# Adding squared outputs to their running sums by an accumulating DMA from GpSimd, in place of GpSimd additions

## The chip, the cores and the metric

The kernel runs on one core of a Trainium2 chip. A core has five engines with queues of their own: TensorE (PE, with its weight loads shown apart as PEld), VectorE (DVE), ScalarE (ACT), GpSimd (POOL) and SyncE (SP, which here only issues DMAs). Sixteen DMA engines move data between the core's memory and HBM. The metric is device time in microseconds (us), the median over several executions. Everything is float32.

## The reference

The reference is one transformer layer on a batch of 2 sequences of 512 tokens with 512 features. A layernorm is followed by two branches that are added to the input: a linear attention with 32 heads of 128, and a base linear layer with a router over 8 low-rank experts. What matters here is the end of the attention branch:

```
attn = blocks of linear attention, heads side by side   # [2, 512, 32*128]
xf   = attn * rsqrt(mean(attn*attn, axis=-1) + EPS)     # mean over all 4096 features of a token
normed = norm_w * xf
gate = sigmoid(hidden @ gate_w.T)
return gate * normed @ out_w.T
```

The mean square of a token runs over all heads, so it is known only when the last head is done. The kernel therefore multiplies the un-normed outputs by `out_w`, sums the squares on the side, and scales the rows at the very end.

## The kernel before, in words

**Stages.** Up to some 45 us the layernorm, the router and the base layer run. After that come the projections as rounds of 7 by 7 smaller products (Strassen's scheme used twice): first the v and gate weights (to about 400 us), whose results go to HBM (`v_kept`, `gate_kept`), then the q and k weights. The attention of a (head, batch) pair starts when its q and k are complete and is woven between the rounds; the product with `out_w` begins within that stage and fills the rest, from about 939 us on.

**One attention item.** There are 64 items, one for each head and batch `b`. `attend` (L685 to L767) is a generator whose parts are run at fixed slots of the round loop (L894 to L960). Its steps are these. v is loaded (L691). The key tile is transposed in 32 by 32 squares by DVE (L697, L698), written to HBM (L702, `k_kept`) and read back as `kt` by four DMAs (L707): this completes the transposition. PE makes the scores (L715), DVE masks them (L720, L724), POOL makes `qd` (L727), and the gate is loaded (L731). ACT scales `kt` to `kd` (L736), PE multiplies `kd` and v (`ps_sc<-v,kd`, by the helper at L99), and DVE makes the states of the blocks (L744, L746). PE then makes the output `pa` in the one PSUM bank with the tag `at` (L749 to L754), and DVE multiplies it by the gate into `gT` (L756). ACT squares `pa` into `sq` (L763), and POOL adds `sq` to `ssq[b]` (L764). For the first item of each batch ACT writes the square into `ssq[b]` itself (L760), so the addition is done 62 times. Last, `gT` is written to HBM (L766, `g_kept`).

**Buffers.** `sq` has one buffer (`RING` at L83, "sq": (1, 1)) of 128 by 512 float32, 256 KB: the next Square may write only when the previous addition has read it. `ssq[0]` and `ssq[1]` are kept for the whole kernel. The items of a batch mostly come in pairs. The bank `at` is single too, so the next item's `pa` waits for this item's Square.

**What sets the order.** Between L372 and L1016 the order on PE, ACT, DVE, POOL and SP is the order in which the code is written; behind that the framework's planner orders the instructions itself. The framework sets the waits. An engine works its queue in order, so an instruction that waits holds up all that stands behind it. On POOL these are the operand sums of the rounds (`s` at L172 and L184, `e` at L191 to L197), `qd` and the sums of `out_w` (`wsum`, L834). All DMAs of this stage are issued by SP; POOL issues none.

**After the last item.** DVE transposes both `ssq` (L1035) and reduces them (L1036), SP sends the parts through HBM (L1038, L1040), and DVE and ACT make `rms`, which the `finish` steps use. DVE also makes the sums `gsum` (L833) that PE's last products read.

Of the kernel before, what the change touches and what calls it, by code (L numbers as in the profile page):

```python
# [37 lines left out]
ALU = mybir.AluOpType  # L38
# [23 lines left out]
def attn_moe_kernel(ctx: ExitStack, tc: tile.TileContext, x, qk_w, v_w, gate_w, out_w, norm_w,  # L62
                    decay, base_w, base_b, router_a_w, lora_b, out):
    nc = tc.nc
# [20 lines left out]
    def ring(tag, shape=None):  # L85
        n, bufs = RING[tag]
        return work.tile(shape or [P, n * 512], F32, tag=tag, name=tag, bufs=bufs)
# [14 lines left out]
    ssq = [keep.tile([P, S], F32, tag=f"ssq{b}", name=f"ssq{b}") for b in range(B)]  # L102
# [574 lines left out]
    def complete(item):  # L677

        items.append(item)
        g = running[len(items) - 1] = attend(*item)  # L680
        ready[len(items) - 1] = now[0] + 4
        for slots in (1, 2, 3, 6):
            later[now[0] + slots].append(g)

    def attend(head, b):  # L685
# [72 lines left out]
        if b not in seen:  # L758
            seen.add(b)
            nc.scalar.activation(ssq[b], pa, AF.Square)  # L760
        else:
            sq = ring("sq")
            nc.scalar.activation(sq, pa, AF.Square)  # L763
            nc.gpsimd.tensor_tensor(ssq[b], ssq[b], sq, ALU.add)  # L764
        yield
        nc.sync.dma_start(g_kept[head // 2][:, :, head % 2, b, :], gT.rearrange("p (f s) -> p f s", f=2))  # L766
        yield  # L767
# [399 lines left out]
```

## Time and profile before

| what | value |
|---|---|
| median of 3 runs | 1118.93 us (1117.61 to 1119.57) |
| the profiled execution | 1121.18 us, of it 1119.4 us span from first to last instruction |
| PE busy | 1106.9 us, 99% of the span |
| DVE, ACT, POOL busy | 773.3, 444.9, 765.7 us |
| the 62 additions on POOL (L764) | 79.2 us, 1277 ns each, the first at 441.5 us, the last at 939.4 us |
| the 62 Squares on ACT (L763) | 597 ns each |
| SP's queue of DMAs | 199.03 MB, 57.9% of 16 engines' span |
| DMA share from 441 to 939 us | 0.65 |

A group's row in the profile has the line, the engine, the operation, the tiles written and read, the shapes and the count; then busy time in us and the mean of one in ns; then the idle time of the engine just before these instructions, with what ended it. A row of the timeline has the start and the length in us, and in square brackets the idle time ahead of it and its releaser. SPq marks DMA issues of SP; their length is that of the issue, and the data land later.

### The profile page before, as it was taken

To read this page: it belongs to the slowest core of one execution; us is meant where nothing else is said; L and a number is where in the kernel's file an instruction comes from. 1 tells how busy PE (TensorE), PEld (TensorE's weight loads), DVE (VectorE), ACT (ScalarE), POOL (GpSimd) and SP (SyncE) were. 2 spreads that over 40 slices of the span, in tenths; PEclk is the share of its full clock that TensorE was granted. 3 is DMA by queue.
4 is the path that set the end of the run, shared out by engine and by line. 5 is a ranking of instruction groups with operands and counts; after the bars stand their busy time and mean duration, and the time that the engine had idled before them with its cause. 6 is when DMAs were issued, how large, how long until landed. Compare 5 with 4: busy or idle time off the path is not lost.

```text
span 1119.4 us, 30341 instructions
## 1 busy us (share of the span) xinstructions
PE 1106.9 (99%) x11984; PEld 849.9 (76%) x11984; DVE 773.3 (69%) x1535; ACT 444.9 (40%) x842; POOL 765.7 (68%) x825
## 2 busy tenths in 40 slices
PE   8999999999999999999999899999999999999998
PEld 7666777777777777777777678777777877777776
DVE  8777776676766668787877777778777786535424
ACT  4344444434444444444444443535444443410000
POOL 3568778779768776677687676777777667545542
PEclk9999999999999999999999999999999999999999
DMA  5534576776743546665665666657666677944221
GB/s 178 156 114 159 163 241 202 220 229 209 239 143 132 177 146 197 182 199 154 199 187 160 191 183 186 189 164 211 181 197 177 211 234 233 350 132 127 86 90 57
DMA packets 190925, 201.09 MB, mean 180 GB/s; under 512 B 53696, under 2 KB 163008, under 8 KB 190656
## 3 DMA queue, kind: packets, MB, share of 16 engines
q1 hardware_dynamic: 190640, 199.03, 57.9%
q8 instruction: 95, 1.56, 0.6%
q14 instruction: 46, 0.38, 0.1%
q10 hardware_dynamic: 144, 0.13, 0.0%
HBM read 128.79 MB, written 75.55 MB: 183 GB/s over the span
## 4 chain that ended last, share of the span: by engine, by line
PE 79%; DVE 10%; DMA 4%; issue 3%; ACT 3%; SPq 1%; POOL 1%; DVEq 0%; ACTq 0%; POOLq 0%
PE sd L99 28%; PE ps_fr L99 24%; PE ps_sc L99 17%; PE ps_at L99 8%; PE ps_sc L715 2%; DVE qk L537 2%; DVE sum L537 2%; DMA raw<-in_qk_w 1%; ACT sd L569 1%; ACT qk L514 1%; DVE w L552 1%; DMA k_kept<-squares 1%; DMA v<-v_kept 1%; DVE gT L756 1%; DVE y L552 0%
## 5 line engine op out<-in xcount | busy, mean ns | idle before, releaser
L99 PE MATMUL sd<-xt,e 128*64 128x256 f32 x1344 | 175.8, 379 | 0.0
L764 POOL TENSOR_TENSOR ssq<-ssq,sq 128x512 f32<-128x512 f32 x62 | 79.2, 1277 | 138.0 <-ACT sq L763 131.0
L514 ACT ACTIVATE qk<-qk 128x512 f32<-128x512 f32 x128 | 80.3, 630 | 203.5 <-DVE qk L537 203.5
L99 PEld LDWEIGHTS sd<-xt,e 128*64 128x64 f32 x1344 | 102.6, 137 | 35.3 <-issue 2.6
L552 DVE TENSOR_TENSOR w<-sd,sum 128x512 f32<-128x512 f32 x110 | 74.5, 690 | 61.0 <-ACT sd L569 60.9
L569 ACT COPY sd<-sd 128x512 f32<-128x512 f32 x112 | 64.2, 573 | 130.1 <-PE sd L99 106.5
L558 ACT COPY sd<-ps_fr 128x512 f32<-128x512 f32 x112 | 64.2, 573 | 72.3 <-PE ps_fr L99 71.2
L99 PE MATMUL ps_at<-scores,v 128*64 128x128 f32 x1024 | 89.6, 273 | 0.0
L834 POOL TENSOR_TENSOR wsum<-wo 128x256 f32<-128x256 f32 x48 | 38.5, 821 | 68.7 <-PE sd L99 28.6
L833 DVE TENSOR_TENSOR gsum<-gated 128x256 f32<-128x256 f32 x54 | 27.3, 546 | 80.9 <-PE ps_sc L99 57.4
L172 POOL TENSOR_TENSOR s<-raw 128x1024 f32<-128x1024 f32 x32 | 75.7, 2367 | 6.8 <-DMA raw<-in_v_w 3.3
L99 PE MATMUL ps_at<-qd,state 128*64 128x128 f32 x768 | 75.2, 273 | 0.0
L99 PE MATMUL ps_fr<-xsum,s 128*64 128x256 f32 x576 | 75.1, 379 | 0.0
L99 PEld LDWEIGHTS ps_at<-scores,v 128*64 128x64 f32 x1024 | 65.9, 138 | 9.1 <-issue 0.4
L756 DVE SCALAR_TENSOR_TENSOR gT<-gate,ps_at 128x512 f32<-128x512 f32 x64 | 43.7, 682 | 36.1 <-PE ps_at L99 34.4
L727 POOL TENSOR_TENSOR qd<-qk,mask 128x384 f32<-128x384 f32 x64 | 64.7, 1010 | 0.9 <-PE ps_at L99 0.9
L191 POOL TENSOR_TENSOR e<-s 128x256 f32<-128x256 f32 x64 | 46.7, 730 | 23.7 <-PE sd L99 21.4
L715 PEld LDWEIGHTS ps_sc<-qk 128*64 128x64 f32 x1024 | 53.6, 137 | 8.7
L763 ACT ACTIVATE sq<-ps_at 128x512 f32<-128x512 f32 x62 | 37.0, 597 | 55.5 <-DVE gT L756 55.5
L99 PE MATMUL sd<-e,xt 128*64 128x256 f32 x448 | 59.0, 379 | 0.0
L99 PE MATMUL ps_fr<-xt,e 128*64 128x256 f32 x440 | 57.7, 382 | 0.2 <-DVE qk L537 0.2
L191 POOL TENSOR_TENSOR e<-raw 128x256 f32<-128x256 f32 x48 | 36.1, 753 | 30.7 <-PE sd L99 30.7
(349 smaller groups left out, 2959.6 us busy)
## 6 DMA issues: line engine op xcount, KB each, us to landing
raw<-in_qk_w SPq DMA_DIRECT2D x64, 256.0 KB
v<-v_kept SPq DMA_DIRECT2D x64, 256.0 KB
gate<-gate_kept SPq DMA_DIRECT2D x64, 256.0 KB
g_kept<-gT SPq DMA_DIRECT2D x64, 256.0 KB
gated<-g_kept SPq DMA_DIRECT2D x27, 512.0 KB
k_kept<-squares SPq DMA_DIRECT2D x64, 192.0 KB
kt<-k_kept SPq DMA_DIRECT2D x256, 48.0 KB
gate_kept<-v SPq DMA_DIRECT2D x47, 256.0 KB
```

Source lines behind the costliest of these rows:

```text
L99: nc.tensor.matmul(o[h * HP : (h + 1) * HP], lhsT[:, of * HP : (of + 1) * HP], rhs, start=start, stop=stop, **more)
L172: nc.gpsimd.tensor_tensor(t, a, b, op)
L191: nc.gpsimd.tensor_tensor(e[:, 0], a21, a22, ALU.add)
L514: nc.scalar.activation(v, v, AF.Silu)
L537: engine.tensor_tensor(o, halves(v), halves(t), ALU.add)
L552: nc.vector.tensor_tensor(o, v, t, ALU.add)
L558: nc.scalar.copy(st["pb"], st["pa"])
L569: nc.scalar.copy(st["pd"], st["pb"])
L715: nc.tensor.matmul(pc[at * HP : (at + 1) * HP, asked], k[:, keys], q[:, asked], start=True, stop=True, skip_group_check=True)
L727: nc.gpsimd.tensor_tensor(qd, q[:, P:].rearrange("p (j n) -> p j n", j=TB - 1), mask[:, 3:5].rearrange("p h n -> p (h n)").unsqueeze(1).to ...
L756: nc.vector.scalar_tensor_tensor(gT, gate, 1.0, pa, ALU.add, ALU.mult)
L764: nc.gpsimd.tensor_tensor(ssq[b], ssq[b], sq, ALU.add)
```

## The change

For all items but the first of each batch, the POOL instruction that adds `sq` to `ssq[b]` is replaced by a DMA that POOL issues: the DMA engines read `sq`, read `ssq[b]`, and write the sum to `ssq[b]`. The Squares, the buffers and everything else stay as written.

```
         else:
             sq = ring("sq")
             nc.scalar.activation(sq, pa, AF.Square)
-            nc.gpsimd.tensor_tensor(ssq[b], ssq[b], sq, ALU.add)
+            nc.gpsimd.dma_start(ssq[b], sq, accum_op=ALU.add)
         yield
```

The DMA takes over the waits of the addition. It needs the Square that wrote `sq`, and the previous change of `ssq[b]`, which is now a DMA as well. What waited for the addition now waits for the landing of the DMA: the next Square (it reuses `sq`), and DVE's transposes of `ssq` after the last item.

More of the change, by code (lines that the diff above doesn't have):

```diff
@@ L763, in attend @@
             nc.scalar.activation(sq, pa, AF.Square)
-            nc.gpsimd.tensor_tensor(ssq[b], ssq[b], sq, ALU.add)
+            nc.gpsimd.dma_start(ssq[b], sq, accum_op=ALU.add)
         yield
```

## The prediction

> **What bounds the kernel now.** I read the page's busy times first, then the chain that ended last, then the waits of PE and of POOL, and last the timeline where PE does wait.
>
> ```profile
> PE 1106.9 (99%) x11984; PEld 849.9 (76%) x11984; DVE 773.3 (69%) x1535; ACT 444.9 (40%) x842; POOL 765.7 (68%) x825
> PE 79%; DVE 10%; DMA 4%; issue 3%; ACT 3%; SPq 1%; POOL 1%; DVEq 0%; ACTq 0%; POOLq 0%
> L764 POOL TENSOR_TENSOR ssq<-ssq,sq 128x512 f32<-128x512 f32 x62 | 79.2, 1277 | 138.0 <-ACT sq L763 131.0
> ```
>
> PE is the bound, and POOL is 1% of the chain. The third row is what goes: POOL spends 79.2 us on the additions and waits 138.0 us ahead of them for the Squares. POOL is early, so a faster POOL only waits longer. PE waits for POOL nowhere in the attention stage; the waits of PE from 441 to 939 us are these.
>
> ```profile
> PE ps_sc L99 <- ACT kd L736: 2.5, 1, 2.5
> PE ps_fr L99 <- ACT sd L558: 2.1, 7, 0.3
> ```
>
> The first is the only large one. It ends a chain of DMAs: `k_kept`, `kt`, then `kd` on ACT. The timeline shows it, SP first, then ACT, then PE.
>
> ```profile
> 624.47 0.55 SPq L702 DMA_DIRECT2D k_kept<-squares  x1
> ...
> 631.41 1.76 SPq L707 DMA_DIRECT2D kt<-k_kept  x4
> ```
> ```profile
> 635.12 0.80 ACT L736 ACTIVATE kd<-kt,mask 128x256 f32<-128x256 f32 x2 [3.63 <-DMA kt<-k_kept]
> ```
> ```profile
> 635.68 0.95 PE L99 MATMUL ps_sc<-v,kd 128*64 128x128 f32 x12 [2.51 <-ACT kd L736]
> ```
>
> `k_kept` took 6.9 us from issue to landing (SP sat until 631.41 for it), `kt` 3.6 more, and PE stood still. The chain repeats every 65.92 us (the double `qk` addition of DVE stands at 491.11, 557.03 and 622.95 us), but the next is at 693.35: this set took 70.40, a slip of 4.5 us for a gap of 2.5 to 3.0. The rest is the clock: from 636 to 640 us its granted share was 0.60.
>
> In other sets the same chain is just in time. By the recorded DMA semaphores `kt` lands at most 0.2 us ahead of its `kd` in 10 items, and the slack that is left to PE behind these is: 0.0 and 0.2 us (items near 566 and 574), 0.1 (622), none (635), 1.0 (643), 0.9 (709), 0.0 (768), 0.8 (841), 1.1 (907), 0.5 (930).
>
> **The change part by part.**
>
> *POOL.* Removed: 62 x 1.277 = 79.2 us. Added: 62 DMA issues, each of d us. No row shows a DMA issued by POOL. From below: SP's issue of `k_kept`, median 0.336 us. From above: the longest common POOL instruction, 128x1024 at 2.367 us. I take 1.0, an estimate between the two, nearer SP's as it is the same kind of work. Behind the issue on POOL stand `qd`, `e` and `wsum`. POOL idles 136.1/61 = 2.2 us ahead of each addition in this stage, which covers 2.367 - 1.277 = 1.1 more, so the cost is 0 at both ends. Were the cover gone, POOL (352.8 busy of 498 us, 77.9 of it these additions) would be full at 352.8 - 77.9 + 61d = 498, d = 3.7 us.
>
> *DMA traffic.* Added: 62 x 0.262 MB. SP's queue moved 199.03 MB in 57.9% of 16 engines' 1119.4 us, so 256 KB hold 16 engines for 0.85 us: the lower bound. The destination is read as well, so I double it for the upper, 1.7, and take 1.3. The stage's DMA share rises from 0.65 by 61 x 1.3/498 = 0.16 to 0.81. There is room on average; the price is paid where an accumulating DMA meets `k_kept` or `kt`. It does: the addition at 556.49 lies between the `k_kept` at 555.89 and its `kt` at 561.26, the one at 622.41 2.1 us ahead of the `k_kept` at 624.47, and those at 758.73 and 824.64 lie 0.6 and 1.3 us behind the `k_kept` at 758.09 and 823.33. SP's order doesn't protect the chain, since the new transfer comes from another queue.
>
> With a delay of 1.3 on each tight chain, less its slack, and counting a set once because a stall relieves what follows: 1.3 (566) + 1.3 (622, 635) + 0.4 (709) + 1.3 (768) + 0.5 (841) + 0.2 (907) + 0.8 (930) = 5.8 us. With 0.85: 0.85 x 3 + 0.35 = 2.9. With two meetings of 1.7, so 3.4: 3.4 + 3.4 + 2.5 + 3.4 + 2.6 + 2.3 + 2.9 = 20.5, and gaps of that length also cool the clock (1.5 to 2 us each as at 636), some 8 us more. Below: the timing of the one slip may also turn out well, minus 4.5.
>
> *The new waits.* The next Square waits until the DMA has landed, and the Squares are on ACT ahead of `kd`, `qk` and the scales. The latency L from issue to landing: from below the 16 KB of `part_kept`, issued at 944.22 and landed by 947.26, 3.0 us; from above `k_kept`'s 6.9. I take 4.5, which lies nearer the usual `k_kept` than its worst. In the steady stage Squares are 7.4 to 9.5 us apart, so the wait costs 0 up to L = 6.5 and under 0.4 beyond; PE's next use of the bank `at` is 3 us later (Square done at 556.42, next `pa` at 559.62). The wait of a DMA for the previous one on `ssq[b]` is covered by the same distance. At the end the items come closer:
>
> ```profile
> 931.58 0.60 ACT L763 ACTIVATE sq<-ps_at 128x512 f32<-128x512 f32 x1 [0.83 <-DVE gT L756]
> 935.50 0.60 ACT L763 ACTIVATE sq<-ps_at 128x512 f32<-128x512 f32 x1 [3.32 <-DVE gT L756]
> 938.75 0.60 ACT L763 ACTIVATE sq<-ps_at 128x512 f32<-128x512 f32 x1 [2.66 <-DVE gT L756]
> ```
> ```profile
> 936.14 0.44 PEld L99 LDWEIGHTS ps_at<-scores,v 128*64 128x64 f32 x8 [0.21 <-ACT sq L763]
> 941.32 1.30 DVE L1035 STREAM_TRANSPOSE turned<-ssq 128x512 f32<-128x512 f32 x2 [1.99 <-DMA g_kept<-gT]
> ```
>
> (the first fence is ACT, in the second PE's last item and DVE's transposes). The DMA of the item at 931.58 is issued at 932.26 and lands at 936.8, so the Square of 935.50 slips 1.3 us, and PE, which already waits for this Square without slack, slips the same 1.3. The last Square then waits for the next DMA, to 942.1, and its own DMA lands at 947.3. DVE's transposes stand at 947.3 in place of 941.3, 6.0 late, and with them the `gsum` queued behind. PE is itself 2.1 late by then (1.3, and 0.8 from the chain at 930), and the second of these `gsum`, ready at 944.6, was used at 947.03, so 2.5 us are covered: 6.0 - 2.1 - 2.5 = 1.4 us more stall. `wsum` behind POOL's last issue is late by about the same, beside it. Sum of the tail 1.3 + 1.4 = 2.7. With L = 3.0 it is 0. With L = 6.9 the Square slips 3.7, the transposes come at 954.3, and 13.0 - 3.7 - 2.5 = 6.8 follow: 10.5. The later way of the sums through HBM (`part_kept`, `rms`) isn't needed before the first `finish`, and costs 0; SP's `gated` and `wo` loads behind `part_kept` have some 5 us before their sums are used.
>
> *A rule against the row.* The row is `part_kept`, 3.0 us for 16 KB. The Trainium skill, DMA: Bandwidth & Descriptors, section Anatomy of one DMA, puts a DMA issued by GpSimd at about 2.0 us plus bytes over 436 GB/s, which would be 2.6 us here, an estimate; by it the tail is 0 and the sum 5.8. As the row for a sixteenth of the bytes is longer already, I keep the row. Speaking against the change, SBUF: State Buffer, section SBUF: two separate sides, says that DVE in its two-port modes keeps GpSimd from writing descriptors, 620 ns becoming some 3100 ns; no run here shows it, and 2.5 us more on L would make the tail nearly that of L = 6.9, for a sum of about 16.
>
> **Sum.** 0 + 5.8 + 2.7 = 8.5 us. The profiled execution took 1121.18 us, 2.25 above the median of the runs, so the sum is added to the median: 1118.93 + 8.5 = 1127.4 us, 0.8% slower.
>
> **The rivals.**
> 1. *The transfer is hidden.* DMA engines are 35% idle, and if the new packets fall between the others, the chains move by less than their slacks and L is near 3.0: within 2.2 us, 1119 us. Against it: three chains have no slack.
> 2. *Faster.* A shorter hold on POOL (0.34 for 1.28) ends `s` and `e` 0.9 us earlier, so raw weight buffers come free earlier, SP issues the loads at 622.50 and 623.84 earlier, and `k_kept` at 624.47 finds empty queues. From the point where `kt` lands 3.0 us earlier (632.0) the slip is gone: 1118.9 - 4.5 = 1114.4. Against it: the added bytes use the same engines, and 0.9 is not 3.0.
> 3. *POOL becomes the bound.* With d above 3.7; at d = 5, 61 x 1.3 = 79 us more, 1198. For it only that no row shows d.
> 4. *The queues back up.* Two meetings per chain, cold clock and L = 6.9: 20.5 + 8 + 10.5 = 39 us, 1158. For it: SP already waits 134.2 us for `k_kept`, so each delay holds back all its other loads.
>
> **How the numbers follow.** What can be told from no change is 0.2%, 2.2 us. Forecast (2 to 20 us slower) 0.60; rival 1 0.15; rival 2 0.08; rival 3 0.06; rival 4 0.11. Faster is rival 2, 0.08; same rival 1, 0.15; slower the rest, 0.77. The forecast's own range is 1121 to 1139. For 8 in 10 I leave out rival 3, rival 2 and the upper part of rival 4: 1117.5 to 1148.
>
> **What would show it.** POOL's idle ahead of what was L764, still some 2 us an item, and no PE wait on POOL. A new DMA queue with about 16 MB and a DMA share near 0.8 in the stage. More rows of `kd` waiting for `kt`, and of PE for `kd`, spaced 66 us, with the granted clock down behind them. Near 936 us a Square that waits for a DMA and PE for that Square, and `turned` waiting for the accumulation. It is wrong if PE waits for `qd` or `e` (d is large), if no new gap appears (the traffic is hidden), or if the gaps sit elsewhere.

## The result: 5.7% slower, and the profile after

The changed kernel takes 1182.58 us (median of 4 runs, 1181.06 to 1184.96) against 1118.37 us before (4 runs, 1117.61 to 1119.57): a ratio of 1.0574, 95% interval 1.0554 to 1.0594. The forecast was 1127.4 us and its range ended at 1148. The profiled execution took 1181.25 us with a span of 1179.4 us, 60.0 us more than the span before.

The page of the changed kernel: busy times, the queue of GpSimd's DMAs, the chain by engine, and the row of the issues (count | busy us, mean ns | idle before, releaser).

```profile
PE 1130.0 (96%) x11984; PEld 884.9 (75%) x11984; DVE 813.8 (69%) x1535; ACT 445.6 (38%) x842; POOL 741.2 (63%) x825
...
q0 software_dynamic: 8928, 16.26, 8.1%
...
PE 80%; DVE 10%; issue 3%; DMA 3%; ACT 2%; SPq 1%; POOL 1%; DVEq 0%; ACTq 0%; POOLq 0%
...
L764 POOL DMA_DIRECT2D ssq<-sq x62 | 54.5, 879 | 221.7 <-ACT sq L763 201.3
```

POOL has less to do and waits longer, as foreseen, and is still 1% of the chain. But DVE is 40.5 us busier, although the change touches no instruction of DVE's. The waits of PE (us in total, times, longest) say where that matters:

```profile
PE ps_fr L99 <- DVE qk L537: 35.6, 13, 4.5
PE ps_sc L99 <- ACT kd L736: 3.7, 2, 3.4
```

Before, the first of these was

```profile
PE ps_fr L99 <- DVE qk L537: 0.2, 1, 0.2
```

and the second, on which the forecast rested, has hardly moved (2.5 us in one wait). So the gaps are new ones, and they wait for `qk` of DVE. One form of `qk` accounts for it. These are the groups of DVE by form; first before, then after.

```profile
L537 DVE TENSOR_TENSOR qk<-w,sum 128x512 f32<-128x512 f32 x8 | 9.7, 1211 | 0.8
```
```profile
L537 DVE TENSOR_TENSOR qk<-w,sum 128x512 f32<-128x512 f32 x8 | 51.5, 6442 | 0.8
```

The same eight instructions take 41.8 us more, as much as all of DVE's extra time. They are the additions that `put` makes with `in_sbuf=True`, at the end of one round in each set of rounds: `w` and `sum` both lie in SBUF, while DVE's other additions of the q and k rounds take one operand from PSUM, and none of their groups has grown. Six of the eight last 8.35 to 8.37 us each; one comes before the first item, and one in the seventh set takes 0.69. That one arrives 0.05 us behind the start of an issue, the six 0.32 us behind it.

The timeline around the second set, before and then after (start, length in us, engine and line, idle time ahead and its releaser):

```profile
556.49 1.28 POOL L764 TENSOR_TENSOR ssq<-ssq,sq 128x512 f32<-128x512 f32 x1 [4.47 <-ACT sq L763]
...
557.03 1.29 DVE L537 TENSOR_TENSOR qk<-w,sum 128x512 f32<-128x512 f32 x1
...
557.73 1.73 POOL L537 TENSOR_TENSOR sum<-w,sum 128x512 f32<-128x512 f32 x1
```
```profile
566.86 0.88 POOL L764 DMA_DIRECT2D ssq<-sq  x1 [4.79 <-ACT sq L763]
567.19 8.37 DVE L537 TENSOR_TENSOR qk<-w,sum 128x512 f32<-128x512 f32 x1
...
567.47 1.57 POOL L537 TENSOR_TENSOR sum<-w,sum 128x512 f32<-128x512 f32 x1
...
568.71 1.01 POOL L191 TENSOR_TENSOR e<-raw 128x256 f32<-128x256 f32 x1
...
572.40 2.60 POOL L172 TENSOR_TENSOR s<-raw 128x1024 f32<-128x1024 f32 x1
...
575.48 0.68 DVE L537 TENSOR_TENSOR qk<-ps_fr,sum 128x512 f32<-128x512 f32 x1
...
576.21 1.98 PE L99 MATMUL ps_fr<-xnT,raw 128*64 128x256 f32 x8 [4.49 <-DVE qk L537]
```

Before, DVE's addition arrives inside POOL's addition, which ends at 557.77, and is done at 558.32. After, it arrives 0.33 us behind the start of the issue. POOL then works through seven instructions without a pause (those left out are `qd` and three more of `e`), until 575.00; DVE's addition ends at 575.56. All of DVE's work waits behind it, the next addition empties a PSUM bank that PE needs, and PE stands still for 4.49 us and 1.43 more. Then the granted clock (PEclk) is down to 0.50. The stretches that follow, each with its length, then busy time and count of PE, PEld, DVE, ACT and POOL, then PEclk, DMA share and GB/s:

```profile
560.00:571.70 11.70, 11.70 (x156) 9.92 (x151) 11.48 (x17) 2.40 (x5) 6.91 (x9) 1.00 0.83 220
571.70:576.20 4.50, 0.02 (x1) 0.00 (x0) 4.50 (x3) 0.61 (x2) 3.30 (x3) 0.80 0.51 156
576.20:580.00 3.80, 2.35 (x10) 1.09 (x12) 3.37 (x10) 1.60 (x4) 0.00 (x0) 0.50 0.81 249
580.00:584.00 4.00, 4.00 (x22) 2.47 (x20) 2.92 (x8) 2.95 (x7) 1.36 (x2) 0.50 0.30 106
```

PE is busy 6.35 us at half clock, which loses 3.2. With the two gaps, 5.9, that is 9.1 us for one set. The six sets from 492.50 to 942.26 us take 449.76; six at 65.92, the usual set of before, would be 395.5, so the price is 54.2 us, or 9.0 each.

The whole: the start to the first of these additions is 1.4 us later; from the first to the seventh the kernel takes 449.8 in place of 400.0, 49.8 more (the 54.2, less the one slip of 4.5 that the kernel before had here); and from the seventh to the end 237.1 in place of 228.3, 8.8 more. Sum 60.0.

The 8.8 at the end hold the waits that the forecast named. ACT's and DVE's waits for the new DMA, and issue to landing of all 62:

```profile
ACT sq L763 <- DMA ssq<-sq: 17.8, 5, 6.8
```
```profile
DVE turned L1035 <- DMA ssq<-sq: 6.0, 1, 6.0
```
```profile
DMA to landing us min/median/max: 3.3/5.0/8.9
```

### The profile page after: what moved, and what is told of

The parts are those of the page before. It is cut to its first block, busy times and chain, and to the rows that moved or that the text cites. A ratio compares the mean times of both kernels' runs of the same rounds, so it can differ in the third digit from the quotient of the medians.

```text
span 1179.4 us, 30428 instructions
## 1 busy us (share of the span) xinstructions
PE 1130.0 (96%) x11984; PEld 884.9 (75%) x11984; DVE 813.8 (69%) x1535; ACT 445.6 (38%) x842; POOL 741.2 (63%) x825
## 3 DMA queue, kind: packets, MB, share of 16 engines
q0 software_dynamic: 8928, 16.26, 8.1%
## 4 chain that ended last, share of the span: by engine, by line
PE 80%; DVE 10%; issue 3%; DMA 3%; ACT 2%; SPq 1%; POOL 1%; DVEq 0%; ACTq 0%; POOLq 0%
PE sd L99 27%; PE ps_fr L99 25%; PE ps_sc L99 15%; PE ps_at L99 8%; DVE qk L537 5%; PE ps_sc L715 3%; DMA k_kept<-squares 1%; DVE sum L537 1%; DMA ssq<-sq 1%; DMA kt<-k_kept 1%; DVE gT L756 1%; PE ps_sc L95 1%; ACT sd L569 1%; PE sd L95 1%; SPq L707 1%
## 5 line engine op out<-in xcount | busy, mean ns | idle before, releaser
L764 POOL DMA_DIRECT2D ssq<-sq x62 | 54.5, 879 | 221.7 <-ACT sq L763 201.3
L99 PE MATMUL sd<-xt,e 128*64 128x256 f32 x1344 | 181.8, 388 | 0.0
L99 PEld LDWEIGHTS sd<-xt,e 128*64 128x64 f32 x1344 | 107.4, 140 | 35.9 <-issue 6.4
L99 PE MATMUL ps_fr<-xnT,raw 128*64 128x256 f32 x384 | 60.9, 442 | 26.9 <-DVE qk L537 26.9
L172 POOL TENSOR_TENSOR s<-raw 128x1024 f32<-128x1024 f32 x32 | 79.1, 2471 | 8.0 <-PE ps_fr L99 4.6
L727 POOL TENSOR_TENSOR qd<-qk,mask 128x384 f32<-128x384 f32 x64 | 77.7, 1213 | 0.8 <-PE ps_at L99 0.8
L99 PE MATMUL ps_fr<-xt,e 128*64 128x256 f32 x440 | 63.3, 409 | 8.8 <-DVE qk L537 8.8
L99 PEld LDWEIGHTS ps_fr<-xnT,raw 128*64 128x64 f32 x384 | 33.6, 159 | 41.6 <-DVE qk L537 28.3
L191 POOL TENSOR_TENSOR e<-raw 128x256 f32<-128x256 f32 x48 | 42.2, 879 | 30.2 <-PE sd L99 30.2
```

Source lines behind the costliest of these rows:

```text
L99: nc.tensor.matmul(o[h * HP : (h + 1) * HP], lhsT[:, of * HP : (of + 1) * HP], rhs, start=start, stop=stop, **more)
L172: nc.gpsimd.tensor_tensor(t, a, b, op)
L191: nc.gpsimd.tensor_tensor(e[:, 0], a21, a22, ALU.add)
L727: nc.gpsimd.tensor_tensor(qd, q[:, P:].rearrange("p (j n) -> p j n", j=TB - 1), mask[:, 3:5].rearrange("p h n -> p (h n)").unsqueeze(1).to ...
L764: nc.gpsimd.dma_start(ssq[b], sq, accum_op=ALU.add)
```

## The experiments

Theory 1 after the result: a DMA that GpSimd issues opens a stretch in which DVE's addition with two SBUF operands isn't let in. Rival: the 16 MB of traffic delay something that DVE or POOL needs. Theory 2: what the forecast priced, late `kt` and late landings, is there too but hidden, since a PE that is 9 us late in each set finds `kt` in time.

### The DMA with hardly any traffic, and without the accumulation

```
-            nc.gpsimd.dma_start(ssq[b], sq, accum_op=ALU.add)
+            nc.gpsimd.dma_start(ssq[b][:, :1], sq[:, :1], accum_op=ALU.add)
```

> The DMA that POOL issues adds one column of the square instead of 512 (the rest of the sums is left out), so the issue on POOL and its place stay, and 16 MB of transfers go. Theory (the issue): once POOL has issued a DMA, the POOL instructions behind it leave VectorE no place for an addition with both operands in SBUF, so the addition qk<-w,sum still takes 8.3 to 8.4 us in six sets, the sets still take 74 to 75 us, and only the 9 us of the end go: 1170 to 1176 us. Rival (the traffic): the data of the transfer hold VectorE's operands up, so without them that addition takes at most 1.3 us and the whole 1118 to 1122 us.

Measured: 1180.53 us, ratio 1.0540 (1.0515 to 1.0566). The traffic fell from 16.26 to 0.04 MB and the time stayed. The additions of this run, by form:

```profile
L537 DVE TENSOR_TENSOR qk<-w,sum 128x512 f32<-128x512 f32 x8 | 56.9, 7110 | 0.8
```

They last longer in all than in the changed kernel, since here the seventh is held too, for 6.06 us. The six sets take 449.3 us (449.8 in the changed kernel), and the stretch behind them 237.3 (237.2). The 9 us that were expected to go at the end stayed: the landings there are shorter (3.4 us in the median of all 62, in place of 5.0), but one hold is added, and the run doesn't part the two. So traffic isn't what holds DVE. The full transfer as a plain copy, without the addition:

```
-            nc.gpsimd.dma_start(ssq[b], sq, accum_op=ALU.add)
+            nc.gpsimd.dma_start(ssq[b], sq)
```

> The changed kernel with its 62 DMAs as plain copies (the square overwrites the sum, so the sums of squares are not formed; the addition of VectorE stays on VectorE). Theory A: VectorE is held by the run of GpSimd instructions that follows an accumulating issue, in which each starts some 0.3 us before the recorded end of the one before (e rows of 1.00 us in place of 0.73); behind plain issues those rows were 0.73 us, so here the addition takes 0.7 to 2.5 us, the sets are 66 to 71 us apart, and the time is that of the plain copies with the addition moved, 1130 to 1143 us. Rival B: any DMA that GpSimd issues does it: the addition takes some 8.4 us in most sets, the sets are some 75 us apart, and the time is 1172 to 1183 us.

Measured: 1182.72 us, ratio 1.0525 (1.0491 to 1.0560). The narrower theory fell. In its place stands its rival: any DMA that GpSimd issues does it (count: shortest/median/longest in ns). Seven of the eight are held here, six for some 8.07 us and the last for 5.78.

```profile
L537 DVE TENSOR_TENSOR qk<-w,sum x8: 691/8068/8081, 425.8 to 939.5; 128x512 f32<-128x512 f32 x8
```

### The addition taken out of the way

The held addition is moved to POOL's own queue, in the changed kernel and, as a control, in the kernel before:

```
-            for (_, to), t in zip(adds, more):
+            for (_, to), t in list(zip(adds, more))[:: -1 if in_sbuf and kind(n) == 2 else 1]:
...
-                    engine = nc.gpsimd if new and in_sbuf else nc.vector
+                    engine = nc.gpsimd if in_sbuf and (new or kind(n) == 2) else nc.vector
```

> The changed kernel, with the one addition of the q and k stage that has both operands in SBUF (qk<-w,sum) done by POOL instead of VectorE; the accumulating DMAs stay whole. Theory (the issue holds VectorE's two-operand addition up): no VectorE instruction over 2 us is left in that stage, the sets take 65.9 us, and what stays is the end (9 us) and up to 6 us of late kt: 1122 to 1134 us. Rival (the traffic, or the wait for kt): another instruction is late instead, sets of 72 us or more, 1165 us and up.

> Control: the kernel before with the same addition given to POOL. Both theories: PE stays the bound, 1116 to 1122 us; if POOL's extra 1.3 us a set mattered, it would be over 1125 us.

Measured: 1157.41 us, ratio 1.0341 (1.0300 to 1.0382); the control 1123.18 us, ratio 1.0023 (1.0008 to 1.0037). The move itself costs 0.2%. In the changed kernel it wins back 2.3%, not the whole, and the time lies between the two expected ranges: no addition of DVE's is held now, but the waits for `kt` have come up that the held PE had hidden. ACT's and PE's waits in it:

```profile
ACT kd L736 <- DMA kt<-k_kept: 33.3, 15, 4.2
```
```profile
PE ps_sc L99 <- ACT kd L736: 18.1, 10, 3.1
```

The kernel before has 6.6 us in 5 waits and 2.5 in one. The second way to part the two leaves the addition on DVE and puts the issue behind POOL's sums of the same slot, so that DVE comes while POOL is in its own sum, with no issue ahead of it:

```
             nc.scalar.activation(sq, pa, AF.Square)
-            nc.gpsimd.dma_start(ssq[b], sq, accum_op=ALU.add)
+            issues.append((ssq[b], sq))
+            if past:
+                issue()
...
         if begun is False:
             next(stage)
             credit -= 1
+        issue()
```

> The changed kernel, with the accumulating DMA issued at the end of its slot, behind the slot's sums on POOL, so that VectorE's qk<-w,sum meets POOL's own addition and not the issue. Theory (the issue): the addition takes 0.7 to 2.0 us, sets of 65.9 us, 1122 to 1134 us. If any POOL instruction at that place did it, or the traffic did, it would still take over 5 us: 1165 us and up.

Measured: 1150.81 us, ratio 1.0292 (1.0232 to 1.0352). The addition took 1.79 us in place of 8.36, and `kd` waited 25.8 us for `kt` in 11 times. The addition fell as expected and the time didn't (1122 to 1134 us expected): two ways of removing the hold agree on what is left, some 3%.

### Hold and traffic one by one

> The one-column DMA (the rest of the sums is left out) together with qk<-w,sum on POOL: the issue on POOL stays, the traffic goes, and VectorE has no two-operand addition that can be held up. The revised theory has two prices: the issue's hold on VectorE (54 us in the changed kernel) and the delay of kt by the traffic, which showed only when the first was gone (sets of 70 to 71.4 us). By it sets of 66.5 us as in the control, hardly a kd that waits for kt, and 2 to 5 us for the longer landings at the end: 1123 to 1130 us. If the issue itself also delayed kt, over 1140 us.

This is the DMA of one column with the addition moved to POOL: 1125.98 us, ratio 1.0073 (1.0047 to 1.0098), as expected. ACT's wait for `kt` in it (the profiled execution was the slowest of six, 1132.63 us):

```profile
ACT kd L736 <- DMA kt<-k_kept: 4.9, 2, 3.7
```

> The kernel with qk<-w,sum on POOL, and the DMA as a plain copy of the square over ssq (the adding is left out): the same issue and the same bytes written, without reading the destination. A packet of 2 KB took 188 ns with the adding and 109 ns as a copy on SP's queue. Theory (kt is late by the time that the transfers hold the DMA engines): about 0.58 of the 30 us that lie between 1157 and 1126, so 1140 to 1148 us. If what counts is that there are data on a second queue at all, 1154 to 1160 us; if the copy is cheap enough for the slack, 1126 to 1132 us.

And this is the plain copy with the addition moved: 1137.70 us, ratio 1.0157 (1.0123 to 1.0192), below its expectation. That took the copy to hold the engines 0.58 times as long as the accumulation; it holds them 0.70 us in place of 1.52, 0.46 times (worked out below). Its queue, against 8.2% of the same column for the accumulating DMA with the addition moved:

```profile
q0 software_dynamic: 4960, 16.26, 3.8%
```

All against the kernel before, as ratios:

| GpSimd's DMA | addition on DVE | addition on POOL |
|---|---|---|
| 256 KB, accumulating | 1.0574 (the change) | 1.0341 |
| 256 KB, plain copy | 1.0525 | 1.0157 |
| one column, accumulating | 1.0540 | 1.0073 |
| none (POOL adds) | 1 | 1.0023 |

Read down the second column: without the hold the accumulating transfer costs 0.0341 - 0.0073 = 2.7%, some 30 us, and the plain copy only 0.8%. Per DMA the 16 engines are held for 0.082 x 1152.2 / 62 = 1.52 us when it accumulates and 0.038 x 1137.3 / 62 = 0.70 when it copies. Read down the first: with the hold the traffic is worth 0.3%, within the intervals. The changed kernel has six held additions there and the two below it seven, so the six sets alone are the cleaner measure: 449.8 us, 448.3 with the plain copy and 449.3 with one column. Read across: the hold is worth 4.7% (52 us, seven additions) where traffic is small and 2.3% (six) where it is full. The two prices hide each other, because a PE that is late anyway doesn't mind a `kt` that is late: `kd` waits for `kt` 5.4 us in 3 times in the changed kernel and 33.3 in 15 without the hold.

### What holds the addition

Two runs keep the addition on DVE and break POOL's run by a copy of one column of `qk`, which must wait for the addition. In the first the two additions of `put` are written in reverse order, as above, so that the copy stands directly behind the issue and ahead of POOL's own sum; in the second it stands behind that sum.

```
                     engine.tensor_tensor(o, halves(v), halves(t), ALU.add)
+                    if in_sbuf and not new and kind(n) == 2:
+                        nc.gpsimd.tensor_copy(seen_by_pool, o[:, 0, :1])
```

> The changed kernel, with the two additions of that slot in the other order and a POOL copy of one column of the new qk right behind the DMA issue: POOL must wait for VectorE's addition there, so its run of instructions breaks. Theory (VectorE waits for POOL's unbroken run): the addition takes 0.7 to 1.5 us, sets near 70 us from the late kt that is left, 1145 to 1160 us. If VectorE waited for the landing of the DMA (5.0 us median) instead, it would take 5 us or more and the whole 1165 us and up.

> The same copy, but behind POOL's own addition of the slot, so the run is one instruction longer before POOL must wait. Theory: VectorE's addition takes 2.2 to 2.8 us, as long as the rest of the issue (0.5) and the addition (1.2) plus its own 0.7. If the length of POOL's run doesn't set it, it is as in the run before this one, or 8.4 us.

Measured: 1153.08 us, ratio 1.0304 (1.0285 to 1.0322), and 1162.28 us in one execution. The timelines, with the copy first, then behind the sum:

```profile
563.22 0.88 POOL L767 DMA_DIRECT2D ssq<-sq  x1 [4.80 <-ACT sq L766]
...
563.54 0.69 DVE L538 TENSOR_TENSOR qk<-w,sum 128x512 f32<-128x512 f32 x1
...
564.30 0.18 POOL L540 COPY seen_by_pool<-qk 128x1 f32<-128x1 f32 x1 [0.20 <-DVE qk L538]
```
```profile
565.34 0.88 POOL L767 DMA_DIRECT2D ssq<-sq  x1 [4.80 <-ACT sq L766]
565.66 2.42 DVE L538 TENSOR_TENSOR qk<-w,sum 128x512 f32<-128x512 f32 x1
...
565.95 1.57 POOL L538 TENSOR_TENSOR sum<-w,sum 128x512 f32<-128x512 f32 x1
...
568.14 0.18 POOL L540 COPY seen_by_pool<-qk 128x1 f32<-128x1 f32 x1 [0.62 <-DVE qk L538]
```

Both as expected, with one exception: in the second run one of the seven additions behind an issue (at 704.44 us) took 0.69 us, although the issue and POOL's sum stand at the same distances from it. What let it through isn't shown. During the issue itself DVE isn't held: 0.69 us in all seven of the first run. It is held by what POOL runs behind the issue, for as long as POOL doesn't stop.

That left open whether the moment of DVE's arrival decides. One reduction of `pd` (PSUM, one column out) ahead of the addition lets it arrive inside POOL's sum, in the changed kernel; two of them do the same in the kernel before, where no DMA is issued:

```
                 nc.vector.tensor_tensor(c, st["pd"], st["y"], ALU.add)
+                if kind(n) == 2:
+                    nc.vector.tensor_reduce(delayed, st["pd"], axis=AX.X, op=ALU.max)
                 put(3, c, addends(3), in_sbuf=True)
```

> The changed kernel with a reduction of pd (PSUM, 128x512, one column out, result unused) put on VectorE right ahead of the addition of each round that holds it, so that the addition reaches VectorE some 0.6 us later: behind the DMA issue, while GpSimd is inside its own sum. Theory A: what matters is the moment of arrival; an addition that arrives while GpSimd is inside an instruction is let in at the end of that one, as in the kernel before (1.29 us). Then it takes 0.7 to 2.0 us, nothing is held for 8 us, the late kt are left, and the time is 1148 to 1165 us. Rival B: after an issue VectorE is let in only when GpSimd idles, whenever it arrives: the addition takes 7.3 to 8.0 us in six sets, the sets stay near 75 us, and the time is 1176 to 1188 us.

> The kernel before, with GpSimd's additions and no DMA of GpSimd's, and two reductions of pd (PSUM, one column out, result unused) on VectorE right ahead of the addition, so that it arrives some 1.35 us later: while GpSimd is inside its own sum, the second instruction after its idle time, with the rest of its run queued behind. Theory A: no issue is needed; any unbroken run of GpSimd's holds the addition until GpSimd idles, and the kernel before escaped since its addition arrived within the first instruction of the run. Then the addition takes 5 to 15 us, PE waits for qk once or more a set, and the time is 1160 to 1260 us. Rival B: the issue is what makes the run closed: here the addition is let in at the end of the sum, 1.0 to 2.0 us, and the time is 1118 to 1132 us.

Measured: 1183.66 us, ratio 1.0548 (1.0508 to 1.0589), and 1127.35 us, ratio 1.0086 (1.0060 to 1.0111). Both theories A fell. The changed kernel with the late arrival, then the kernel before with it:

```profile
567.73 1.57 POOL L538 TENSOR_TENSOR sum<-w,sum 128x512 f32<-128x512 f32 x1
567.86 7.94 DVE L538 TENSOR_TENSOR qk<-w,sum 128x512 f32<-128x512 f32 x1
...
572.65 2.59 POOL L172 TENSOR_TENSOR s<-raw 128x1024 f32<-128x1024 f32 x1
```
```profile
560.91 1.28 POOL L538 TENSOR_TENSOR sum<-w,sum 128x512 f32<-128x512 f32 x1
...
561.34 1.39 DVE L538 TENSOR_TENSOR qk<-w,sum 128x512 f32<-128x512 f32 x1
562.15 1.18 POOL L191 TENSOR_TENSOR e<-raw 128x256 f32<-128x256 f32 x1
```

The addition arrives 0.13 and 0.43 us into the same `sum`, with the same run of POOL's behind it. Without an issue it is let in at the end of that instruction; behind an issue only when the whole run is over. In every one of these timelines it ends 0.54 to 0.56 us after the POOL instruction that it waited for: 558.32 against 557.77 (before), 562.73 against 562.19 (before, late), 568.08 against 567.52 (copy behind the sum), 575.56 against 575.00 (changed), 575.80 against 575.24 (changed, late). The changed kernel with the late arrival also has the case without an issue: its first addition comes ahead of the first item, 0.44 us into the same `sum`, and is let in at the end of that one.

```profile
427.40 1.38 DVE L538 TENSOR_TENSOR qk<-w,sum 128x512 f32<-128x512 f32 x1
```

Nor is it how early in an instruction DVE comes: in the kernel before, a `gsum` with two SBUF operands that comes 0.02 us into a `wsum` (at 966.88), with the next `wsum` close behind, takes 1.00 us and is done 0.28 us behind the first one's end. So it is an issue ahead of the run that closes it to DVE. That is shown for an addition that arrives late in the issue or inside the first instruction behind it; this addition wasn't made to arrive later than that.

A second form does the same in the changed kernel, behind the sets. `s<-raw` of DVE (128x256, two SBUF operands) arrives at 959.81, 1.16 us behind the start of an issue. It isn't let in where POOL goes from `qd` to `e` without a gap, and is done 0.30 us behind the end of that `e`, where POOL pauses for 0.08 us.

### The end

With the addition on POOL, the last squares are added by POOL again (seven of them by the code; the expectation says 8):

```
+            squared.append(sq)
+            if len(squared) < 56:
                 nc.gpsimd.dma_start(ssq[b], sq, accum_op=ALU.add)
+            else:
+                nc.gpsimd.tensor_tensor(ssq[b], ssq[b], sq, ALU.add)
```

> The kernel with qk<-w,sum on POOL and whole accumulating DMAs, but POOL's additions again for the last 8 squares. Theory: the end (the last Squares that wait for landings, and the last kt) costs 8 to 9 us, so 1157.4 becomes 1147 to 1151 us, and near the end no Square waits for a DMA. If those waits were covered by late loads anyway, 1155 to 1158 us.

Measured: 1145.01 us, ratio 1.0246 (1.0217 to 1.0276), against 1.0341 with the DMA to the end: 1.0%, some 11 us. It is more than expected, but the run also has fewer late `kt` (28.9 us of waits in place of 33.3), so it bounds the landing waits from above. The two profiled executions part it: behind the seventh addition the run takes 232.4 us in place of 237.9, 5.5 less, and the other 4.9 lie in the six sets (416.6 in place of 421.5), whose code is the same. The control takes 228.3 behind the seventh addition.

## Why the prediction was wrong

**The sign** was right and the number far off: 64 us slower measured, 8.5 forecast, 29 at the end of the range.

**The step that failed** is *POOL*: "Behind the issue on POOL stand `qd`, `e` and `wsum` ... so the cost is 0 at both ends". It asked how long the issue holds POOL, and that part was right: an issue is recorded with 0.876 us in the median where 1.0 was taken, POOL waits for Squares as before, and PE never waits for `qd` or `e`. It didn't ask who else is held while POOL works behind an issue. That costs 54.2 us of span in the six sets, and no term or rival had it. A trace of before had the hint: the one addition with two SBUF operands took 1.29 us where a POOL addition ran beside it and 0.69 without one. It was used only as a mark for counting sets.

Of the rules that bore on this, the prediction weighed the wrong one. Six additions of 8.36 us behind POOL's instructions are the rows; the Trainium skill, SBUF — State Buffer, section SBUF: two separate sides, says that a VectorE instruction with two SBUF inputs and a GpSimd instruction that reads SBUF exclude each other, and that whoever starts first keeps the other out for the whole instruction. The runs agree on the pair, and with "instruction" for the kernel before (1.29 and 1.39 us); behind an issue it is a run of seven instructions, and there the measurement decides.

**DMA traffic**: forecast 5.8 us, bounds 2.9 and 20.5 with 8 more for a cold clock. The mechanism was right. In the changed kernel it is hidden (449.8 us for the six sets, 449.3 with hardly any traffic). Where the hold is gone, traffic and landing together cost 2.7%, some 30 us. By the profiled executions, against the control, the six sets take 22.4 us more (421.5 and 399.1) and the end 9.6 (237.9 and 228.3), so the chains cost the upper bound, not the value taken. The time of one transfer wasn't the error (1.52 us measured, 1.3 taken); the delay of each `kt` was. Without the hold `kd` waited up to 4.2 us for it, in 15 items (5 before), and PE up to 3.1 us for `kd`, where 1.3 was added for one meeting. Rival 4, with two meetings per chain, a cold clock and late landings, gave 39 us; without the hold these two stretches are 32 longer.

**The new waits**: landing took 5.0 us in the median (4.5 taken), but 8.9 at the worst, beyond the upper bound of 6.9. The predicted places were right: five Squares between 941 and 1000 us waited 0.5 to 6.8 us, and `turned` 6.0. With POOL's additions for the last seven squares the end is 5.5 us shorter in the profiled executions (11 in all by the medians), where 2.7 was forecast and 10.5 was the bound. The rule weighed there, of the Trainium skill, DMA: Bandwidth & Descriptors, section Anatomy of one DMA, would give 2.6 us for 256 KB; the 62 landings of the changed kernel have a minimum of 3.3 (the plain copies 2.3, with a median of 3.7), so keeping the row was right.

**Rivals 1 to 3.** The transfer isn't hidden once the hold is gone. The slip at 632 us did vanish, as rival 2 has it, and gave back 4.5 us of 54.2. But it vanished in the control too, which has no DMA of POOL's (seven additions 66.5 us apart), so it doesn't speak for rival 2. POOL didn't become the bound. The signs were named rightly in one point: "if the gaps sit elsewhere". They do.

## What to carry to other kernels

When work moves to a DMA that GpSimd issues, list every VectorE instruction that reads two operands from SBUF and see what GpSimd runs behind the issue: here six of seven such instructions waited for all of it, 8.4 us in place of 1.3. Either issue where GpSimd stops soon after, or put that VectorE operation on another engine. And when a fix wins back less than the gap it removes, look for a second wait that the first had covered; the table with both causes on and off shows it, and no single run does.

## What the runs showed of the hardware that was not expected

- Behind a DMA issue of GpSimd's, whether accumulating, plain, of 256 KB or of one column, a VectorE addition with two SBUF operands was let in only when GpSimd paused: 8.36, 8.07, 7.94 or 6.06 us. Two got through in 0.69: one that came 0.05 us behind the start of the issue, and one at the usual 0.32. Without an issue it was let in between two instructions of the same run (1.29 and 1.39 us). Why the issue makes this difference isn't settled by the runs; VectorE's additions with one operand in PSUM showed nothing of it.
- An accumulating issue is recorded with 0.876 us, for 256 KB and for one column alike, a plain one with 0.577. GpSimd's next instruction starts some 0.6 us behind the start of either.
- Behind an accumulating issue GpSimd's rows overlap in the profile: `e` is recorded with 1.00 us in place of 0.73, while the starts stay 0.69 us apart. Behind plain issues `e` is recorded with 0.73, and the hold is nearly the same (8.07 us), so the overlap isn't its cause.
- An accumulating DMA takes 16 engines 1.52 us for 256 KB and lands 5.0 us after its issue in the median; a plain copy takes 0.70 and lands after 3.7.
